# An LSTM kernel on Trainium2: the additions of its 32-step cycle laid out anew, and a head of 48 steps with a tail of 16

## The chip, the cores and the metric

The kernel runs on one core of one Trainium2 chip. A core has four compute engines that the document names as the profile does: PE (matrix multiplication, with its weight loads listed as PEld), DVE, ACT and POOL. The queue SP issues nearly all DMAs. PE writes its results to a memory of its own, PSUM; all engines reach the main on-chip memory, SBUF. The metric is the device time of one execution in microseconds; the lower, the better.

## The reference

One LSTM layer runs over 512 steps for a batch of 32, with 512 inputs and 512 hidden units, all in float32; the input is added to the output at the end:

```python
xW = jnp.einsum('ntd,dg->ntg', x, Wx) + b      # x: 32 x 512 x 512, Wx: 512 x 2048
def step(carry, xw_t):
    prev_h, prev_c = carry
    a = xw_t + prev_h @ Wh                      # Wh: 512 x 2048
    i, f, o = sigmoid of the first three quarters of a; g = tanh of the last
    next_c = f * prev_c + i * g
    next_h = o * jnp.tanh(next_c)
(_, _), hs = jax.lax.scan(step, (h0, c0), jnp.swapaxes(xW, 0, 1))
return x + jnp.swapaxes(hs, 0, 1)
```

The products `prev_h @ Wh` have to be done one step after the other. The products `x @ Wx` depend on no step and can be done at any time before the step that uses them.

## The kernel before, in words

**A step.** The loop `for k in range(T)` at the end of the kernel writes out the order of all work by hand; every engine keeps the order in which its instructions are issued. Step k first issues `h_part(k)`, the 64 matmuls `prev_h @ Wh` (line L745), which add onto gate sums in PSUM. Then comes one *window* of other work, number v = k + 4, and then `cell(k)`: three activations on ACT (L782 to L784), three DVE instructions (L785 to L787), the last tanh on ACT (L788), the product h = o * tanh(c) on DVE (L789), and its transpose on DVE (L790), for which the next `h_part` waits. POOL adds the residual (L843) and the result is stored. ACT copies the x products of the next steps into the gate banks (`seed_first`, L730, and `seed_last`).

**The x products.** Steps are taken in rows of eight (`ROW`). The first row is multiplied directly (`direct`, L660, and `keep_direct`, L676). Four rows at a time, 32 steps, form a cycle of `PER` = 32 windows. For one cycle the product `x @ Wx` is made by a fast scheme with R = 26 block products; each block product is in turn made of seven smaller ones (two levels of sums, like Strassen's). `A_OPS` holds the sums of rows ("nodes", L398), `C_OPS` the sums of products that give the 16 output blocks in `C_OF`. Each of the seven smaller products is a group of eight matmuls (L463), issued by `products(v)`. The factors of the weights are made during the head and kept in DRAM; `fetch` loads them into two rings, wa and wb (tags `wa`, `wb`), for each product. The function `begin(n)` says in which window of the cycle product n begins; it spans a few windows, so each window issues groups of several products: six groups in most windows, five in some. Four to five windows after its beginning, `finish_product` takes the two halves of a product out of PSUM.

**The sums on DVE.** In `evacuate(v)`, ACT copies parts of the products in the works (L492, L496, L505, L506) and DVE adds others (L499, L507). Sums of finished products come in two kinds. *Half adds* (L619, 128x512) are issued at once, in the window in which a half of a product is ready; these read the half in PSUM. A product that is used later as well (`copied`) is copied to SBUF by ACT in two halves (L607). *Full adds* (L635, 128x1024) read SBUF only and are put in a queue, `due`, with the window by which they must be done. A set `at_half` holds the sums that are made as half adds: those that read a product just finished, what these feed, and those whose limit leaves less than two windows. `limit` goes back from the outputs: `SLACK` gives, for each of the four rows of a cycle, how many windows after the last product its sums may be done. A sum lives in a *slot*; `slot` takes one from the list `free`, `used` gives it back after the last use. Finished outputs are stored to DRAM (`store`), and `load_xw` loads them back three steps ahead of their use; POOL adds the bias (`add_bias`, L707).

The queue `due` also holds the node sums (L398, 128x512) and the four short adds of each product (L426 to L429, 128x128). `run_due(v, room)` walks it in order: what is due by window v is issued in any case, what is due later only while `room`, counted in columns plus `FIXED` for each instruction, lasts:

```python
            if window > v and (columns + FIXED > room or not ready(v)):
                i += 1
                continue
            assert ready(window)
            due.pop(i)
            fn()
            room -= columns + FIXED
```

It is called three times in a window: twice in `evacuate`, with `FIRST_SUMS` ahead of the finishing of products and with at most `BETWEEN` ahead of the last copies, and once after it with what remains of `ROOM`. `AHEAD` says how many windows ahead of a product's beginning its sums enter the queue.

**Head and tail.** The first `HEAD` = 40 steps are the head. Its rows 1 to 4 are made by a simpler seven-product scheme, four *units* a row, 14 groups each; a window holds one unit or none, and the units are spread over the windows before `START` = 21, in which the first cycle begins. `LEAD` = 23 sets `START`: a cycle's first window is issued in step HEAD - LEAD of the first cycle, LEAD steps ahead of the first step that uses it (`START = windows_of(HEAD - LEAD)[0]`). `NSB` = 14 cycles follow. The last `TAIL` = 24 steps are multiplied directly, in quarters of a step (`tail_products`): one quarter a window at first, then two and three in turn (`2 + v % 2`), 96 in all. From step `HALVES` = 466 on, when the cycles' products are done, the step itself runs in two halves (`h_halves`, L759, and `cell_halves`, L804 to L830).

## Time and profile before

| | |
|---|---|
| three runs | 3178.97, 3179.61, 3184.61 us |
| their median | 3179.61 us |
| the profiled execution | 3181.38 us |
| its span | 3179.4 us |
| granted PE clock over the span | 1.00 |
| PE busy | 3114.2 us, 98% of the span |
| DVE busy | 2404.0 us, 76% |
| ACT busy | 1645.9 us, 52% |
| POOL busy | 1065.0 us, 33% |

The span runs from the first instruction of the profiled execution to its last. Times are in microseconds unless marked ns. Engine names stand as above; L12 is line 12 of the kernel. A line of a list of instructions gives the start, the duration, the engine, the line, the operation, what it writes and reads ("out<-in"), and the shapes as partitions x elements; "x8" stands for eight like instructions in a row, and a bracket at the end names what the engine waited for. In a table of groups, the busy time, the mean of one in ns, the idle time just ahead and what ended most of it follow the bar. In a table of windows, each engine has its busy time and count, and the last three columns are the granted clock, the share of the DMA engines and GB/s.

### The profile page before, as it was taken

To read this page: it belongs to the slowest core of one execution; us is meant where nothing else is said; L and a number is where in the kernel's file an instruction comes from. 1 tells how busy PE (TensorE), PEld (TensorE's weight loads), DVE (VectorE), ACT (ScalarE), POOL (GpSimd) and SP (SyncE) were. 2 spreads that over 40 slices of the span, in tenths; PEclk is the share of its full clock that TensorE was granted. 3 is DMA by queue.
4 is the path that set the end of the run, shared out by engine and by line. 5 is a ranking of instruction groups with operands and counts; after the bars stand their busy time and mean duration, and the time that the engine had idled before them with its cause. 6 is when DMAs were issued, how large, how long until landed. Compare 5 with 4: busy or idle time off the path is not lost.

```text
span 3179.4 us, 133096 instructions
## 1 busy us (share of the span) xinstructions
PE 3114.2 (98%) x55992; PEld 1977.0 (62%) x55992; DVE 2404.0 (76%) x6428; ACT 1645.9 (52%) x5090; POOL 1065.0 (33%) x993
## 2 busy tenths in 40 slices
PE   9999999999999999999999999999999999999998
PEld 5666666565665656666566665666666666666555
DVE  6747877878777787787877878788787877878444
ACT  2455455554555555555555555555555555554333
POOL 0223333333333333333333333333333333333310
PEclk9999999999999999999999999999999999999999
DMA  8756767767676686766867767676676767767200
GB/s 288 254 189 209 250 213 226 237 211 255 210 247 218 216 259 202 252 216 213 263 196 254 221 216 251 210 250 222 216 254 210 249 217 227 236 213 240 88 29 25
DMA packets 338853, 687.71 MB, mean 216 GB/s; under 512 B 44368, under 2 KB 112976, under 8 KB 337744
## 3 DMA queue, kind: packets, MB, share of 16 engines
q1 hardware_dynamic: 338112, 679.20, 66.1%
q8 instruction: 441, 7.23, 0.9%
q14 instruction: 156, 1.28, 0.1%
q10 hardware_dynamic: 144, 0.01, 0.0%
HBM read 499.46 MB, written 179.57 MB: 214 GB/s over the span
## 4 chain that ended last, share of the span: by engine, by line
PE 76%; DVE 15%; DMA 5%; issue 2%; ACT 2%; SPq 0%; DVEq 0%; ACTq 0%
PE gates L745 39%; PE pp L463 12%; PE acc L463 12%; PE gates L759 5%; PE p L463 4%; DVE raw_sb L619 3%; DVE t L619 2%; DMA wb<-keep_b 2%; PE pp L660 2%; DMA xw<-xw 1%; DMA wa<-keep_a 1%; DVE t L635 1%; DVE c L787 1%; DVE slot_h L619 1%; PE acc L660 1%
## 5 line engine op out<-in xcount | busy, mean ns | idle before, releaser
L745 PE MATMUL gates<-wh_sb,ht 128*32 128x384 f32 (+1 forms) x29760 | 1703.5, 379 | 20.1 <-DVE ht L790 18.4
L745 PEld LDWEIGHTS gates<-wh_sb,ht 128*32 128x32 f32 x29760 | 1022.5, 110 | 719.9 <-issue 603.9
L843 POOL TENSOR_TENSOR oc<-xr,ht 128x128 f32<-128x128 f32 x509 | 407.5, 801 | 2015.6 <-DVE ht L790 1749.1
L707 POOL TENSOR_TENSOR xw<-xw,bias_sb 128x512 f32<-128x512 f32 x480 | 673.4, 1403 | 82.0 <-DMA xw<-xw 57.3
L782 ACT ACTIVATE s<-gates 128x256 f32<-128x256 f32 x466 | 180.0, 386 | 554.5 <-PE gates L745 553.9
L785 DVE TENSOR_TENSOR fc<-s,c 128x128 f32<-128x128 f32 x465 | 139.9, 301 | 222.1 <-ACT s L782 221.3
L463 PE MATMUL pp<-wb,nodes 128*32 128x256 f32 x3808 | 304.7, 379 | 0.0
L505 ACT COPY pp<-pu 128x512 f32<-128x512 f32 x380 | 228.4, 601 | 101.2 <-DVE t L619 38.3
L789 DVE TENSOR_TENSOR fc<-s,ig 128x128 f32<-128x128 f32 x466 | 137.4, 295 | 175.9 <-ACT ig L788 175.9
L788 ACT ACTIVATE ig<-c 128x128 f32<-128x128 f32 x466 | 144.9, 311 | 179.6 <-DVE c L787 153.5
L463 PE MATMUL acc<-wb,s 128*32 128x256 f32 x2576 | 206.7, 381 | 22.8 <-DVE s L428 22.8
L730 ACT COPY gates<-xw 128x384 f32<-128x384 f32 x462 | 218.5, 473 | 4.5 <-DVE nodes L676 3.0
L507 DVE TENSOR_TENSOR pp<-acc,p 128x256 f32<-128x256 f32 x380 | 161.7, 425 | 68.5 <-ACT pp L506 65.1
L784 ACT ACTIVATE s<-gates 128x128 f32<-128x128 f32 x466 | 129.8, 279 | 157.1 <-PE gates L745 157.1
L463 PE MATMUL acc<-wa,s 128*32 128x256 f32 x2576 | 205.9, 381 | 2.4 <-DVE pp L507 0.8
L506 ACT COPY pp<-acc 128x256 f32<-128x256 f32 x380 | 136.8, 360 | 134.9 <-DVE t L619 60.9
L463 PE MATMUL pp<-wb,s 128*32 128x256 f32 x2576 | 205.4, 379 | 0.0
L463 PE MATMUL p<-wa,s 128*32 128x256 f32 x2576 | 204.7, 379 | 0.0
L499 DVE TENSOR_TENSOR pu<-acc,p 128x256 f32<-128x256 f32 x380 | 157.6, 415 | 35.9 <-ACT p L496 26.2
L790 DVE STREAM_TRANSPOSE ht<-fc 128x128 f32<-128x128 f32 x466 | 145.2, 312 | 49.7 <-DVE fc L789 1.4
L759 PE MATMUL gates<-wh_sb,ht 128*32 128x256 f32 x2944 | 168.5, 379 | 10.2 <-DVE fc L810 9.4
L759 PEld LDWEIGHTS gates<-wh_sb,ht 128*32 128x32 f32 x2944 | 114.7, 110 | 72.9 <-ACT s L806 20.4
(217 smaller groups left out, 4647.4 us busy)
## 6 DMA issues: line engine op xcount, KB each, us to landing
wb<-keep_b SPq DMA_DIRECT2D x322, 512.0 KB, 5.4
wa<-keep_a SPq DMA_DIRECT2D x322, 384.0 KB, 4.2
xw<-xw SPq DMA_DIRECT2D x480, 256.0 KB, 4.4
xw<-t SPq DMA_DIRECT2D x312, 128.0 KB, 3.1
xw<-raw_sb SPq DMA_DIRECT2D x288, 128.0 KB, 3.2
xr<-in_x_dram SPq DMA_DIRECT2D x256, 128.0 KB, 3.2
out_dram<-oc SPq DMA_DIRECT2D x255, 128.0 KB, 2.8
row<-in_x_dram SPq DMA_DIRECT2D x63, 512.0 KB, 6.9
```

Of the source, the lines that this page charges most:

```text
L463: nc.tensor.matmul(dst[t * B : (t + 1) * B], a[:, t], w, start=s in (1, 5) and m == 0, stop=True, skip_group_check=True,)
L499: nc.vector.tensor_add(job.pu[:, 1], job.acc, job.p5)
L505: nc.scalar.copy(job.pp[0], job.pu)
L507: nc.vector.tensor_add(job.pp[1][:, 1], job.acc, job.p5)
L619: add(v)(sums[sb, v][:, half], source(a), source(b))
L707: nc.gpsimd.tensor_add(xw[t], xw[t], bias_sb)
L730: nc.scalar.copy(gates[t % 2][:, 0:IFG], xw[t][:, 0:IFG])
L745: nc.tensor.matmul(g[j * B : (j + 1) * B, cols], state["ht"][:, k, :], wh_sb[:, k, j, cols], start=False, stop=True, skip_group_check=True,)
L759: nc.tensor.matmul(bank_half(m)[j * B : (j + 1) * B], state["ht"][:, k, :], half(wh_sb[:, k, j], m), start=False, stop=True, skip_group_ch ...
L782: nc.scalar.activation(s[:, 0:2], g[:, 0:2], AF.Sigmoid)
L790: nc.vector.transpose(ht.rearrange("p q b -> p (q b)"), h)
L843: (nc.gpsimd if t < T - 3 else nc.vector).tensor_add(state["oc"][:, tt % 2], xr[t][:, tt % 2], ht)
```

## The change

The change touches how the additions are laid out and how the 512 steps are divided; the matmuls of a cycle, their order and the step's own code stay.

- `HEAD` goes from 40 to 48 steps and `TAIL` from 24 to 16. The number of cycles stays 14. The head gets four more units (row 5); the tail has 64 quarter products for 96, and takes two a window throughout.
- `LEAD` goes from 23 to 28, so that `START` becomes 24 (HEAD - LEAD + 4), `LAST` 470 for 467 and `HALVES` 469 for 466. A cycle begins five steps earlier, counted from the steps that use it.
- `COPIED` names the last three products of a cycle, 23, 24 and 25. They are copied to SBUF by ACT whether or not a later sum needs that, and sums that read them are no longer made as half adds for that reason.
- `SLACK` goes from [1, 1, 1, 3] to [3, 3, 5, 8]: the outputs of the four rows may be done later after the last product of their cycle. Together with `COPIED`, this leaves 48 half adds and 18 full adds in a cycle, for 60 and 12, and three products more are copied out, 13 for 10.
- A sum may take the slot of an operand that it uses up (`last_use`, `moved`): it is then written over that operand, and needs no free slot.
- `run_due` returns what it spent, and `evacuate` counts that against the window's room, where it had counted the whole of `FIRST_SUMS` or `BETWEEN`. `ROOM` goes from 3400 to 4300, `FIRST_SUMS` from 1000 to 1200, `BETWEEN` from 1200 to 1300, and `AHEAD` from 3 to 5.
- In a cycle, `load_row` is issued eight windows ahead, where it was six; the tail loads two rows, where it loaded three.

```diff
--- before.py
+++ after.py
@@ -35,21 +35,22 @@
 R = len(A_OF)
 
 PER = ROW * MO
-HEAD = 5 * ROW
-TAIL = 3 * ROW
+HEAD = 6 * ROW
+TAIL = 2 * ROW
 NSB = (T - HEAD - TAIL) // PER
 END = HEAD + NSB * PER
 assert END + TAIL == T
 
-LEAD = 23
+LEAD = 28
 NODES = 10
 FIXED = 160
-ROOM = 3400
-FIRST_SUMS = 1000
-BETWEEN = 1200
+ROOM = 4300
+FIRST_SUMS = 1200
+BETWEEN = 1300
 HEAD_ROOM = 5000
-SLACK = [1, 1, 1, 3]
-AHEAD = 3
+COPIED = (23, 24, 25)
+SLACK = [3, 3, 5, 8]
+AHEAD = 5
 def rows_by_use():
     found = []
 
@@ -348,17 +349,18 @@
 
     def run_due(v, room):
 
-        i = 0
+        i = spent = 0
         while i < len(due):
             window, _, columns, fn, ready = due[i]
-            if window > v and (columns + FIXED > room or not ready(v)):
+            if window > v and (columns + FIXED > room - spent or not ready(v)):
                 i += 1
                 continue
             assert ready(window)
             due.pop(i)
             fn()
-            room -= columns + FIXED
+            spent += columns + FIXED
             i = 0
+        return spent
 
     nodes, node_uses = {}, {}
     node_pairs = [const.tile([P, 2, ROW, 2, B], F32, name=f"nodes_{i}") for i in range(NODES // 2)]
@@ -479,9 +481,7 @@
                     job.release()
 
     def evacuate(v, room):
-        before = len(due)
-        run_due(v - 0.5, FIRST_SUMS)
-        taken = FIRST_SUMS if len(due) < before else 0
+        taken = run_due(v - 0.5, FIRST_SUMS)
         for half, late in ((1, 5), (0, 4)):
             job = jobs.get(v - late)
             if job:
@@ -500,8 +500,7 @@
             taken += C + FIXED
         job = jobs.get(v - 3)
         if job:
-            run_due(v, min(room - taken, BETWEEN))
-            taken += BETWEEN
+            taken += run_due(v, min(room - taken, BETWEEN))
             nc.scalar.copy(job.pp[0], job.pu)
             nc.scalar.copy(job.pp[1][:, 0], job.acc)
             nc.vector.tensor_add(job.pp[1][:, 1], job.acc, job.p5)
@@ -551,7 +550,7 @@
         uses[a] += 1
         uses[b] += 1
         for v, other in ((a, b), (b, a)):
-            if v < R and (v != n or other == v):
+            if v < R and (v != n or other == v or n in COPIED):
                 copied.add(v)
     for v in C_OF:
         uses[v] += 1
@@ -561,7 +560,7 @@
     at_half = set()
     for v in range(len(ready) - 1, R - 1, -1):
         n = ready[v]
-        if n in C_OPS[v - R][1:] or any(ready[u] == n and (u in at_half) for u in users[v]):
+        if (n in C_OPS[v - R][1:] and n not in COPIED) or any(ready[u] == n and (u in at_half) for u in users[v]):
             at_half.add(v)
 
     def done_at(n):
@@ -576,17 +575,27 @@
         )
         if v not in at_half and limit[v] < done_at(n) + 2:
             at_half.add(v)
-    sums, left_uses = {}, {}
+    sums, left_uses, moved = {}, {}, set()
+
+    def last_use(sb, v):
+        return [u for u in (C_OPS[v - R][1:] if v >= R else ()) if left_uses.get((sb, u)) == 1 and u not in C_OF]
 
     def slot(sb, v):
-        sums[sb, v] = free.pop(0)
+        ends = last_use(sb, v)
+        if ends:
+            sums[sb, v] = sums[sb, ends[0]]
+            moved.add((sb, ends[0]))
+        else:
+            sums[sb, v] = free.pop(0)
         left_uses[sb, v] = uses[v]
 
     def used(sb, v):
         if (sb, v) in left_uses:
             left_uses[sb, v] -= 1
             if left_uses[sb, v] == 0:
-                free.append(sums.pop((sb, v)))
+                f = sums.pop((sb, v))
+                if (sb, v) not in moved:
+                    free.append(f)
 
     def put_out(sb, v):
         for at, u in enumerate(C_OF):
@@ -641,7 +650,8 @@
                     START + PER * sb + limit[v] - 0.5,
                     8 * P,
                     go,
-                    lambda at, v=v: len(free) > (at < START + PER * sb + limit[v] - 0.5) and all((sb, u) in sums for u in C_OPS[v - R][1:]),
+                    lambda at, v=v: all((sb, u) in sums for u in C_OPS[v - R][1:])
+                    and (last_use(sb, v) or len(free) > (at < START + PER * sb + limit[v] - 0.5)),
                 )
             return taken
 
@@ -691,7 +701,7 @@
         for t in whole:
             keep_direct(t, tail_banks[(t - END) % 6], tail_room())
         whole.clear()
-        room = 1 if v <= LAST + 3 else 2 + v % 2
+        room = 1 if v <= LAST + 3 else 2
         for t, q in pieces[:room]:
             direct(t, tail_banks[(t - END) % 6], (q,))
             if q == NJ - 1:
@@ -908,7 +918,7 @@
         if job and job.w >= START and streamed(job.kind[1]):
             job.ring[1] = rpool.tile([P, 4, C], F32, name=f"wb_{job.w}", tag="wb", bufs=4)
             nc.sync.dma_start(out=job.ring[1].rearrange("p n c -> p (n c)"), in_=kept[B_AT[job.kind[1]]][1])
-        if v in (LAST - 4, LAST - 2, LAST):
+        if v in (LAST - 4, LAST - 2):
             load_row(END // ROW + (v - LAST + 4) // 2)
         for i in [i for i in range(8) if i not in RESIDENT][2 * (v - LAST) - 2 : 2 * (v - LAST)] if v > LAST else ():
             if i in again:
@@ -917,7 +927,7 @@
             else:
                 raw[i] = rpool.tile([P, 4, C], F32, name=f"raw_again_{i}", tag="wb", bufs=4)
             nc.sync.dma_start(out=raw[i].rearrange("p n c -> p (n c)"), in_=wx[i])
-        sb, rest = divmod(v + 6 - START, PER)
+        sb, rest = divmod(v + 8 - START, PER)
         if v + 6 in UNIT_AT[2 * NJ :: NJ]:
             load_row(3 + UNIT_AT[2 * NJ :: NJ].index(v + 6))
         if rest < MO and 0 <= sb < NSB:
```

## The prediction

> **What bounds the kernel now.** I read the page, then the span in three stretches, then one cycle step by step.
>
> ```profile
> span 3179.4 us, 133096 instructions
> PE 3114.2 (98%) x55992; PEld 1977.0 (62%) x55992; DVE 2404.0 (76%) x6428; ACT 1645.9 (52%) x5090; POOL 1065.0 (33%) x993
> PE 76%; DVE 15%; DMA 5%; issue 2%; ACT 2%; SPq 0%; DVEq 0%; ACTq 0%
> 53.60:186.30 132.70, 132.70 (x2468) 90.25 (x2463) 79.09 (x182) 60.89 (x179) 27.23 (x29) 1.00 0.73 232
> 186.30:2919.30 2733.00, 2684.69 (x49156) 1715.70 (x49148) 2169.99 (x5667) 1476.03 (x4431) 990.69 (x896) 1.00 0.71 228
> 2919.30:3179.40 260.10, 245.00 (x3748) 146.17 (x3744) 119.58 (x504) 100.01 (x461) 46.91 (x64) 0.99 0.20 60
> ```
>
> PE looks full, yet DVE holds 15% of the chain that ended last. The three stretches (length, then busy PE, PEld, DVE, ACT, POOL, clock, DMA) are the head, the 14 cycles (195.2 us each) and the tail.
>
> A step is PE's h products and, in a cycle, six or five groups of eight product matmuls (seven groups for each of 26 products, 182 a cycle). L789 marks each cell.
>
> ```profile
> 1518.40 0.31 DVE L790 STREAM_TRANSPOSE ht<-fc 128x128 f32<-128x128 f32 x1
> 1519.58 3.66 PE L745 MATMUL gates<-wh_sb,ht 128*32 128x384 f32 x64
> 1523.03 0.64 PE L463 MATMUL pp<-t,row 128*32 128x256 f32 x8
> ...
> 1525.62 0.86 PE L745 MATMUL gates<-wh_sb,ht 128*32 128x384 f32 x8
> 1347.42 0.29 DVE L789 TENSOR_TENSOR fc<-s,ig 128x128 f32<-128x128 f32 x1 [0.38 <-ACT ig L788]
> 1367.21 0.29 DVE L789 TENSOR_TENSOR fc<-s,ig 128x128 f32<-128x128 f32 x1 [0.38 <-ACT ig L788]
> 1375.37 0.29 DVE L789 TENSOR_TENSOR fc<-s,ig 128x128 f32<-128x128 f32 x1 [0.38 <-ACT ig L788]
> 1386.73 0.29 DVE L789 TENSOR_TENSOR fc<-s,ig 128x128 f32<-128x128 f32 x1 [0.38 <-ACT ig L788]
> 1392.78 0.29 DVE L789 TENSOR_TENSOR fc<-s,ig 128x128 f32<-128x128 f32 x1 [0.38 <-ACT ig L788]
> ```
>
> PE's prices are 3.45 for the h products (1523.03 - 1519.58) and 0.4317 for a group (2.59 for the six up to 1525.62). A cycle's floor is 32 x 3.45 + 182 x 0.4317 = 189.0 us; a step's is 6.04 with six groups, 5.61 with five. The quiet step from 1386.73 to 1392.78 takes 6.05: at the floor. I number a cycle's windows 0 to 31; the cell at 1367.21 is that of window 1. The four windows 31, 0, 1 and 2 take 1375.37 - 1347.42 = 27.95, the last of them 8.16, against floors of 5.61 + 3 x 6.04 = 23.73. There DVE's bulk of additions sets the step, as window 12 shows:
>
> ```profile
> 1428.17 0.29 DVE L789 TENSOR_TENSOR fc<-s,ig 128x128 f32<-128x128 f32 x1 [0.38 <-ACT ig L788]
> 1428.57 0.31 DVE L790 STREAM_TRANSPOSE ht<-fc 128x128 f32<-128x128 f32 x1
> 1428.81 1.19 DVE L635 TENSOR_TENSOR raw_sb<-raw_sb,t 128x1024 f32<-128x1024 f32 x1
> 1429.92 1.48 DVE L635 TENSOR_TENSOR t<-raw_sb,slot_h 128x1024 f32<-128x1024 f32 x1
> 1431.32 0.68 DVE L619 TENSOR_TENSOR t<-pp,slot_h 128x512 f32<-128x512 f32 x1
> ...
> 1433.95 0.28 DVE L785 TENSOR_TENSOR fc<-s,c 128x128 f32<-128x128 f32 x1
> ...
> 1435.13 0.29 DVE L789 TENSOR_TENSOR fc<-s,ig 128x128 f32<-128x128 f32 x1 [0.38 <-ACT ig L788]
> ```
>
> From the end of L790 (1428.88) to L785 (1433.95) lie 5.07 us of work; the cell with its transpose takes the other 1.89 of the 6.96 from L789 to L789. So a step takes the larger of PE's floor and DVE's work + 1.89. A quiet step has slack in front: ht is there at 1518.71, PE takes it at 1519.58, 0.87 later; about 0.75 of that can be used up once before PE waits.
>
> Busy time hides part of the loss, as the ends of pipelined matmuls are counted: 2733.0 - 2684.7 = 48 us idle, but 2733.0 - 14 x 189.0 = 87 above the floor. I go by the floor. The Trainium skill (Trainium Kernel Development and Optimization, Performance Expectations) calls matmul busy time "a bad metric" for the distance to the best; by busy time the most to be gained in the cycles would be 48 us.
>
> **The change part by part.** *Sums.* Walking the queue of due sums through one cycle, before and after: products copied by ACT 10 and 13, half adds 60 and 48, full adds 12 and 18; node sums (18), short adds (104), L499 and L507 (26 each) stay. The first window behind a full add shows the prices:
>
> ```profile
> 1387.12 0.31 DVE L790 STREAM_TRANSPOSE ht<-fc 128x128 f32<-128x128 f32 x1
> 1387.36 1.18 DVE L635 TENSOR_TENSOR slot_h<-slot,t 128x1024 f32<-128x1024 f32 x1
> 1388.46 0.41 DVE L499 TENSOR_TENSOR pu<-acc,p 128x256 f32<-128x256 f32 x1
> 1388.80 0.28 DVE L428 TENSOR_TENSOR s<-row 128x128 f32<-128x128 f32 x1
> 1388.99 1.38 DVE L427 TENSOR_TENSOR s<-s,nodes 128x128 f32<-128x128 f32 x1
> 1390.29 0.28 DVE L429 TENSOR_TENSOR s<-row,s 128x128 f32<-128x128 f32 x1
> 1390.49 0.28 DVE L428 TENSOR_TENSOR s<-nodes 128x128 f32<-128x128 f32 x1
> 1390.70 0.42 DVE L507 TENSOR_TENSOR pp<-acc,p 128x256 f32<-128x256 f32 x1
> ...
> 1388.83 1.40 POOL L707 TENSOR_TENSOR xw<-xw,bias_sb 128x512 f32<-128x512 f32 x1
> ...
> 1559.45 0.69 DVE L619 TENSOR_TENSOR raw_sb<-raw_sb,t 128x512 f32<-128x512 f32 x1
> 1560.06 0.68 DVE L398 TENSOR_TENSOR nodes<-row 128x512 f32<-128x512 f32 x1
> L607 ACT COPY t<-pp 128x512 f32<-128x512 f32 x116 | 67.6, 583 | 57.7 <-PE pp L463 56.3 <-DMA wb<-keep_b 1.4
> ```
>
> From one start to the next: full add 1.11, half add and node sum 0.61, short add 0.20, L499 or L507 0.34. DVE saves 12 x 0.61 and pays 6 x 1.11: 0.7 us a cycle less. What counts is where the work lies.
>
> A sum written over its own operand: no row has its price. Between 0 and 0.3 a full add (the 1.48 of 1429.92 against 1.19), 0 to 5 us a cycle; a gain is excluded, as the same elements pass. I take 0, the nearest row being the plain add.
>
> One short add, at 1388.99, lasts 1.38 while POOL's bias add L707 runs; an add that reads a product in PSUM (L619 from pp) does not lengthen. So an add with both inputs in SBUF can wait some 1.1 us for POOL, and the change turns PSUM adds into SBUF adds. I keep 1.1 for each window in which two or more short adds follow a node or full add. The Trainium skill has this as a rule (SBUF — State Buffer, Who interferes with whom): a DVE instruction with two SBUF inputs contends with a GpSimd instruction that reads SBUF, and the one fully blocks. By that rule, the trace agrees.
>
> DVE's work after, from the walk. Window 1: node, three shorts, L507, full: 2.7 + 1.1 + 0.3 for POOL's L843 = 4.1. Window 2: full, L499, four shorts, full: 3.4 + 1.1 = 4.5. Window 3: node, L499, four shorts, L507, full: 4.3. Window 4, one short fewer: 4.1. Windows 5 and 6: full, L499, three shorts, L507, full: 3.5 + 1.1 = 4.6 each. Windows 31 and 0 fall to 3.0 and 3.5. So windows 1 to 6 need 26.2 + 6 x 1.89 = 37.5 against floors of 5 x 6.04 + 5.61 = 35.8; less the slack 0.75, 1.0 us stays. In the middle of the cycle a full add joins window 13: windows 11 to 15 hold 4.1, 4.3, 4.7, 4.5, 4.2 = 21.8, with the cells 31.3, against 29.3; less 0.75, 1.2 stays. Every other window holds at most 4.1, and 6.04 - 1.89 = 4.15 fit.
>
> One loss goes with the longer lead. A bias add that came late sat on a cell:
>
> ```profile
> 1540.91 1.29 POOL L707 TENSOR_TENSOR xw<-xw,bias_sb 128x512 f32<-128x512 f32 x1 [3.38 <-ACT s L783]
> ...
> 1541.07 1.27 DVE L787 TENSOR_TENSOR c<-fc,ig 128x128 f32<-128x128 f32 x1
> ```
>
> L787 takes 0.29 elsewhere (the rows' form is the cell's), so 0.98 was lost. Rows of xw are stored as little as 2 windows ahead of their load, after the change 7. What is late next: full adds at the end of a window whose stores hold the one SP queue, and with it the next xw load. Between 0 and 2 us a cycle; I take 0.9, about one such add.
>
> *ACT.* Six copies more, 583 ns each: 3.5 us a cycle, in windows 0 to 3. ACT is busy 1476 of 2733 us, and window 5, with two copies of its own, keeps the floor (the 6.05 above). Cost 0; with that cover gone, up to 3.5 x 14 = 49 us.
>
> *Queues and buffers.* SP issues the same stores, some later; the row load moves two windows ahead, to windows where its buffer's last reader is three windows back. The banks of the last products are freed by ACT's copy, no later than by the adds. ROOM, FIRST_SUMS, BETWEEN and AHEAD only place what is counted above. Cost 0.
>
> *Cycles:* 14 x (189.0 + 1.0 + 1.2 + 0.9) + 4.3 (ten groups that the head leaves over, as now) = 2693.7, against 2733.0.
>
> *Head.* 20 steps for 17 and four units more, 56 groups: 3 x 3.45 + 56 x 0.43 = 34.5. PE is busy 132.7 of its 132.7 us, so nothing covers this. The head ends at 186.3 + 34.5 = 220.8.
>
> *Tail.* 64 quarter products for 96, two to a step.
>
> ```profile
> 3136.55 3.66 PE L759 MATMUL gates<-wh_sb,ht 128*32 128x256 f32 x64
> 3141.72 3.66 PE L759 MATMUL gates<-wh_sb,ht 128*32 128x256 f32 x64
> 3146.55 3.66 PE L759 MATMUL gates<-wh_sb,ht 128*32 128x256 f32 x64 [1.17 <-DVE fc L810]
> ```
>
> A step with two quarters takes 5.17; one with none 4.83, where PE waits for the cell. After: 6.6 and 6.4 for the two steps with the last full adds, 5.6, 30 x 5.17, ten unfilled at 4.85, and 3.4 from the last tanh to the end: 225.6, against 260.1. Head and tail cancel.
>
> Sum: 220.8 + 2693.7 + 225.6 = 3140.1 of span. The profiled execution of before took 3181.38 for its span of 3179.4; the median of its runs is 3179.61, 0.2 above that span. Forecast 3140.
>
> **The rivals.** *Nothing is left over the floor* (0.15): full adds keep POOL back, its bias add comes at another place, and no short add waits. Unlocked, no window holds more than 4.0. Then 220.8 + 14 x 189.0 + 4.3 + 225.6 = 3097. Against it: the 1.38 above.
>
> *Late bias adds* (0.08): the stores at window ends make L707 late three times more a cycle, 0.98 each on a cell: 3 x 0.98 x 14 = 41, so 3181, no change; the change does not do what it says. For it: SP is one queue, in order. Against: the margin of 7 windows.
>
> *POOL's lock takes the gain* (0.09), which ends slower. Short adds move from the front of a window to behind node and full adds, where L707 runs. Work without waiting is 98.8 us a cycle (104 x 0.20 + 66 x 0.61 + 18 x 1.11 + 52 x 0.34), 3.09 a window, 4.98 with the cell; 195.2 / 32 = 6.10 is reached at 1.12 of waiting in every window. At a whole L707 (1.29) everywhere a cycle is 200.6 and the kernel takes 3256. Against: in the window quoted three of four short adds wait for nothing.
>
> **How the numbers follow.** The forecast has 0.68, with 3112 to 3170 as its own range (0.1 to 4.3 us a cycle above or below its 192.1, by the bounds of lock and late stores). The range 3097 to 3176 reaches to the first rival and leaves out the third and most of the second. 0.2% (6 us) is about what a measurement of this kernel can tell. Faster 0.68 + 0.15 + 0.02 = 0.85, same 0.05, slower 0.10, the small parts from the second rival's edges.
>
> **What would show it.** Right: the four windows 31 to 2 near 24.5 instead of 27.95; windows 5 and 6 longer than now, near 6.5; 48 half and 18 full adds a cycle; a cycle near 192; no bias add on a cell. Wrong: short adds above 1 us in most windows; L707 starting beside L785 to L789; L782 late behind ACT's copies in windows 0 to 3; steps of the head above 3.45 + 0.43 a group.

## The result, and the profile after

The changed kernel takes 3135.5 us (median of four runs, 3133.65 to 3136.97), where the kernel before took 3181.5 beside it: a ratio of 0.9855, with a 95% interval from 0.9838 to 0.9872. That is 1.45% faster. The forecast was 3140 and the range 3097 to 3176. The number came out; of the reasons given for it, half did not, as the experiments show.

The page of the changed kernel (first lines, and the chain's shares by engine), and then its span in the same three stretches as in the prediction (length, busy PE, PEld, DVE, ACT, POOL, clock, DMA share, GB/s). The lines of the code have moved: L755 is the old L745, L799 the old L789, L717 the bias add L707, L628 the half adds L619, L644 the full adds L635.

```profile
span 3135.0 us, 133350 instructions
PE 3101.0 (99%) x56184; PEld 1986.8 (63%) x56184; DVE 2421.7 (77%) x6337; ACT 1697.0 (54%) x5186; POOL 1030.9 (33%) x1001
PE 76%; DVE 18%; ACT 3%; issue 2%; DMA 1%; DVEq 0%; SPq 0%; ACTq 0%
```

```profile
53.20:220.90 167.70, 167.70 (x3115) 100.92 (x3108) 89.42 (x215) 77.06 (x222) 35.67 (x35) 1.00 0.66 207
220.90:2906.30 2685.40, 2672.49 (x49143) 1736.00 (x49136) 2187.74 (x5588) 1515.63 (x4509) 940.17 (x896) 1.00 0.72 232
2906.30:3135.00 228.70, 208.94 (x3316) 128.39 (x3307) 109.37 (x460) 95.72 (x436) 54.82 (x66) 1.00 0.23 72
```

The head ends at 220.9 (186.3 before), the tail takes 228.7 (260.1), and the 14 cycles take 2685.4 (2733.0). So all of the gain is in the cycles, 47.6 us, and head and tail together give 3.2 of it back. DVE is busier than before and holds 18% of the chain for 15%. Busy time does not tell its work, as it counts waits for POOL too (see the end); by the prediction's prices the new sums are 0.7 us a cycle less work, and a cycle became 3.5 us shorter.

The timeline of DVE and POOL in one cycle: the cells of windows 30, 2 and 4, and window 5, some rows left out, up to its own cell at 1405.38.

```profile
1362.91 0.29 DVE L799 TENSOR_TENSOR fc<-s,ig 128x128 f32<-128x128 f32 x1 [0.38 <-ACT ig L798]
...
1387.01 0.29 DVE L799 TENSOR_TENSOR fc<-s,ig 128x128 f32<-128x128 f32 x1 [0.37 <-ACT ig L798]
...
1398.97 0.29 DVE L799 TENSOR_TENSOR fc<-s,ig 128x128 f32<-128x128 f32 x1 [0.38 <-ACT ig L798]
1399.37 0.31 DVE L800 STREAM_TRANSPOSE ht<-fc 128x128 f32<-128x128 f32 x1
1399.60 1.18 DVE L644 TENSOR_TENSOR slot_h<-slot_h,raw_sb 128x1024 f32<-128x1024 f32 x1
1400.70 0.41 DVE L499 TENSOR_TENSOR pu<-acc,p 128x256 f32<-128x256 f32 x1
1401.04 0.28 DVE L431 TENSOR_TENSOR s<-row,s 128x128 f32<-128x128 f32 x1
1401.23 1.38 DVE L430 TENSOR_TENSOR s<-nodes 128x128 f32<-128x128 f32 x1
...
1403.07 1.21 DVE L644 TENSOR_TENSOR t<-t,t 128x1024 f32<-128x1024 f32 x1
...
1405.38 0.29 DVE L799 TENSOR_TENSOR fc<-s,ig 128x128 f32<-128x128 f32 x1 [0.37 <-ACT ig L798]
...
1399.76 1.35 POOL L853 TENSOR_TENSOR oc<-xr,ht 128x128 f32<-128x128 f32 x1 [3.50 <-DVE ht L800]
1401.07 1.39 POOL L717 TENSOR_TENSOR xw<-xw,bias_sb 128x512 f32<-128x512 f32 x1
```

Windows 31 to 2 take 1387.01 - 1362.91 = 24.10 us, where they took 27.95 (24.34 and 27.96 in the mean of the cycles). Window 5 takes 6.41 and has become longer (6.05 before): it now holds two full adds and a short add that lasts 1.38 beside POOL's L717. The full adds at 1399.60 and 1403.07 are written over an operand and last 1.18 and 1.21. A row leaves the numbers of the buffers out; by the order in which the code takes its slots, 14 of the 18 full adds of a cycle are written so, and their median is 1.21 us, that of the others 1.20.

For every run below, the same reading of all cycles: the mean cycle (the 2nd to the 14th, from cell to cell) and what its windows take above PE's floor of 5.61 or 6.04. These numbers are worked out from the starts of the cell's product o * tanh(c), L799 or its line in each trace; a window that gains back a little stands below zero. Windows 17 to 26, left out, lie within 0.1 us of the floor in all, but 0.4 below it in e6 and e7. Each ratio is to the kernel before as it ran beside that kernel, and each cycle comes from one trace.

| kernel | time, us | ratio to before | cycle, us | above the floor in windows 30 to 2 | 3 to 10 | 11 to 16 | 27 to 29 | head ends | tail |
|---|---|---|---|---|---|---|---|---|---|
| before | 3179.6 | 1 | 195.07 | 4.86 | -0.24 | 1.43 | 0.02 | 186.3 | 260.1 |
| changed | 3135.5 | 0.9855 | 191.59 | 0.92 | 0.50 | 1.08 | 0.03 | 220.9 | 228.7 |
| e1_room_old | 3181.2 | 1.0001 | 195.16 | 0.38 | 0.03 | 5.59 | 0.14 | 221.0 | 228.5 |
| e2_not_copied | 3136.7 | 0.9855 | 191.59 | 0.81 | 0.59 | 1.08 | 0.10 | 220.8 | 227.3 |
| e3_no_bias | 3100.9 | 0.9747 | 189.07 | 0.01 | 0.03 | 0.02 | 0.02 | 220.9 | 225.6 |
| e4_before_lead | 3185.2 | 1.0013 | 195.11 | 4.79 | -0.16 | 1.44 | 0.01 | 220.9 | 230.0 |
| e5_before_room | 3157.1 | 0.9930 | 193.29 | 2.66 | -0.17 | 1.78 | 0.01 | 186.6 | 260.2 |
| e6_spread | 3127.6 | 0.9835 | 191.03 | 0.42 | -0.06 | 2.06 | 0.05 | 220.7 | 228.0 |
| e7_spread_early | 3115.3 | 0.9798 | 189.99 | 0.23 | -0.14 | 1.05 | 0.25 | 221.1 | 228.4 |
| e8_lead23 | 3133.6 | 0.9855 | 191.78 | 0.70 | 0.84 | 1.21 | 0.02 | 240.2 | 204.5 |
| e9_early | 3134.2 | 0.9852 | 191.45 | 0.67 | 0.43 | 1.27 | 0.07 | 220.8 | 228.7 |
| e10_best | 3113.6 | 0.9787 | 189.84 | 0.03 | 0.03 | 0.77 | 0.01 | 220.9 | 227.9 |
| e11_before_queue | 3184.9 | 1.0006 | 195.57 | 1.90 | 0.20 | 1.14 | 3.33 | 186.3 | 259.2 |
| e12_queue_rows | 3137.2 | 0.9864 | 191.93 | 1.55 | 0.30 | 1.06 | 0.03 | 186.2 | 259.1 |

### The profile page after: what moved, and what is told of

Read it like the earlier page. It is cut to its first block, busy times and chain, and to the rows that moved or that the text cites. A ratio compares the mean times of both kernels' runs of the same rounds, so it can differ in the third digit from the quotient of the medians.

```text
span 3135.0 us, 133350 instructions
## 1 busy us (share of the span) xinstructions
PE 3101.0 (99%) x56184; PEld 1986.8 (63%) x56184; DVE 2421.7 (77%) x6337; ACT 1697.0 (54%) x5186; POOL 1030.9 (33%) x1001
## 3 DMA queue, kind: packets, MB, share of 16 engines
q8 instruction: 442, 7.24, 1.0%
## 4 chain that ended last, share of the span: by engine, by line
PE 76%; DVE 18%; ACT 3%; issue 2%; DMA 1%; DVEq 0%; SPq 0%; ACTq 0%
PE gates L755 39%; PE pp L465 13%; PE acc L465 13%; PE p L465 4%; PE gates L769 4%; DVE t L644 2%; DVE s L430 1%; DVE t L628 1%; DVE raw_sb L644 1%; DVE c L797 1%; ACT ig L798 1%; DVE ht L800 1%; DVE fc L799 1%; PE pp L670 1%; DVE s L428 1%
## 5 line engine op out<-in xcount | busy, mean ns | idle before, releaser
L755 PE MATMUL gates<-wh_sb,ht 128*32 128x384 f32 (+1 forms) x29952 | 1714.5, 380 | 12.0 <-DVE ht L800 9.5
L755 PEld LDWEIGHTS gates<-wh_sb,ht 128*32 128x32 f32 x29952 | 1026.0, 110 | 718.5 <-issue 600.8
L853 POOL TENSOR_TENSOR oc<-xr,ht 128x128 f32<-128x128 f32 x509 | 406.0, 798 | 1997.3 <-DVE ht L800 1794.7
L717 POOL TENSOR_TENSOR xw<-xw,bias_sb 128x512 f32<-128x512 f32 x488 | 640.5, 1313 | 89.9 <-DMA xw<-xw 53.4
L799 DVE TENSOR_TENSOR fc<-s,ig 128x128 f32<-128x128 f32 x469 | 138.3, 295 | 176.3 <-ACT ig L798 176.3
L795 DVE TENSOR_TENSOR fc<-s,c 128x128 f32<-128x128 f32 x468 | 140.8, 301 | 143.8 <-ACT s L792 141.8
L769 PE MATMUL gates<-wh_sb,ht 128*32 128x256 f32 x2752 | 157.5, 379 | 14.7 <-DVE fc L820 14.7
L496 ACT COPY p<-p 128x256 f32<-128x256 f32 x384 | 146.4, 381 | 28.0 <-PE p L465 25.8
```

What stands on the lines that cost most here:

```text
L717: nc.gpsimd.tensor_add(xw[t], xw[t], bias_sb)
L755: nc.tensor.matmul(g[j * B : (j + 1) * B, cols], state["ht"][:, k, :], wh_sb[:, k, j, cols], start=False, stop=True, skip_group_check=True,)
L769: nc.tensor.matmul(bank_half(m)[j * B : (j + 1) * B], state["ht"][:, k, :], half(wh_sb[:, k, j], m), start=False, stop=True, skip_group_ch ...
L799: nc.vector.tensor_mul(h, s[:, 3], tc_t)
L853: (nc.gpsimd if t < T - 3 else nc.vector).tensor_add(state["oc"][:, tt % 2], xr[t][:, tt % 2], ht)
```

## The experiments

### What holds the rest: POOL's bias add

```diff
-            if 2 * 4 - 2 <= k and k + 2 < END:
+            if 2 * 4 - 2 <= k and k + 2 < HEAD:
                 add_bias(k + 2)
```

> The changed kernel without the bias add on POOL (L717) for the steps that the cycles feed; it leaves out the bias of these steps, so the output differs from the reference by that. Theory of the prediction (what stays above PE's floor in windows 1 to 6 and 11 to 16, now 2.6 us a cycle, is DVE's adds blocked while L717 runs): a cycle falls to about 189.1 and the time by 14 x 2.5 = 35 us to 3100 us. Rival (the rest is DVE's work itself, L717 and the adds only happen together): a cycle stays within 0.5 us of 191.6 and the time within 7 us of 3135.5.

3100.9 us, 0.9747 of before (0.9730 to 0.9763). The cycles and the tail of this run, and a window 5 of it:

```profile
220.90:2873.50 2652.60, 2652.14 (x49144) 1760.37 (x49139) 2020.19 (x5589) 1521.26 (x4510) 402.20 (x473) 1.00 0.73 235
2873.50:3099.10 225.60, 209.22 (x3316) 128.30 (x3306) 106.52 (x460) 96.01 (x436) 21.79 (x41) 1.00 0.24 73
```

```profile
1385.09 0.29 DVE L799 TENSOR_TENSOR fc<-s,ig 128x128 f32<-128x128 f32 x1 [0.38 <-ACT ig L798]
...
1387.36 0.28 DVE L430 TENSOR_TENSOR s<-nodes 128x128 f32<-128x128 f32 x1
...
1390.86 0.29 DVE L799 TENSOR_TENSOR fc<-s,ig 128x128 f32<-128x128 f32 x1 [0.38 <-ACT ig L798]
```

The short add that took 1.38 takes 0.28, the window 5.77 for 6.41, and every cycle from the 2nd on falls to 189.07, 0.1 over PE's floor, in all groups of windows of the table. The tail falls by 3.1 as well, to the 225.6 of the prediction. So the whole rest above the floor goes with the bias add. It could also have held up ACT's copies of xw into the gate banks, which read what it writes; but in the changed kernel these waited for it only 1.7 us in all, in 2 places. What remains is that it keeps DVE out. The Trainium skill (SBUF — State Buffer, Who interferes with whom) calls what the two share an exclusive lock; the trace agrees, 1.38 against 0.28.

### What carries the gain: the kinds of sums, or the room

The first run takes only the room back, the second only the three copied products.

```diff
-ROOM = 4300
-FIRST_SUMS = 1200
-BETWEEN = 1300
+ROOM = 3400
+FIRST_SUMS = 1000
+BETWEEN = 1200
```

> The changed kernel with the room of a window as it was before: ROOM 3400, FIRST_SUMS 1000, BETWEEN 1200 (what is spent is still counted exactly). Theory of the prediction (the gain comes from the sums of the last three products, the longer SLACK and the longer lead; the room only places work, cost 0): the time stays at 3135.5 us, within 6 us, and a cycle at 191.6. Rival, the room: with 3400 spent and counted, the full adds no longer fit ahead of their limits and pile up at them. Walking the queue at the prediction's prices gives a pile in windows 11 to 14 (8.5, 6.6, 7.3, 7.1 us) and a cycle of about 194.3, which is 14 x 2.6 = 36 us more: 3172 us.

```diff
-COPIED = (23, 24, 25)
+COPIED = ()
```

> The changed kernel with COPIED empty: products 23 to 25 are no longer copied out, and their sums are half adds again (60 half and 12 full adds a cycle); room, SLACK and lead stay changed. Theory of the prediction (these half adds are what made windows 31 to 2 long): they fall into windows 1 to 4 again and cost at least half of what windows 31 to 2 gained (3.6 us a cycle), so 14 x 1.8 = 25 us more: about 3160 us. Rival, the room: which kind of add it is makes little difference as long as the others can be moved away from them; the walk of the queue gives 192.1 for 192.0 a cycle: 3137 us, no difference that can be measured, with windows 3 and 4 near 6.7 and windows 5 and 6 near 6.0 and 5.5.

With the old room the time is 3181.2, a ratio of 1.0001 (0.9991 to 1.0010): the gain is gone. Without the three copies it is 3136.7, a ratio of 0.9855 (0.9840 to 0.9869): nothing has changed. Window 11 of the run with the old room:

```profile
1449.18 0.29 DVE L799 TENSOR_TENSOR fc<-s,ig 128x128 f32<-128x128 f32 x1 [0.38 <-ACT ig L798]
...
1449.82 1.18 DVE L644 TENSOR_TENSOR slot_h<-slot_h,raw_sb 128x1024 f32<-128x1024 f32 x1
1450.92 1.48 DVE L644 TENSOR_TENSOR raw_sb<-t,raw_sb 128x1024 f32<-128x1024 f32 x1
1452.44 2.19 DVE L644 TENSOR_TENSOR t<-t,slot_h 128x1024 f32<-128x1024 f32 x1
...
1457.68 0.29 DVE L799 TENSOR_TENSOR fc<-s,ig 128x128 f32<-128x128 f32 x1 [0.38 <-ACT ig L798]
...
1451.28 2.26 POOL L717 TENSOR_TENSOR xw<-xw,bias_sb 128x512 f32<-128x512 f32 x1
```

Three full adds that found no room before their limit stand in one window of 8.50 us; the third meets L717 and lasts 2.19. Windows 30 to 2 are at the floor in this run (0.38 above it), just as the prediction's account of the sums would have it, and all of it comes back in windows 11 to 16 (5.59). The rival's walk had 8.5, 6.6, 7.3 and 7.1 for windows 11 to 14; in the mean they took 8.35, 6.70, 7.54 and 6.99 (its 3172 us in all was 9 short). The work that left one crowded place stood in another.

That the second run had other sums is seen in the counts of the half adds of the cycles, of the changed kernel first and then of this run (the columns are those of the stretches, with DVE's L628 alone):

```profile
220.90:2910.00 2689.10, 452.79 (x672) 1.00 0.72 232
```

```profile
220.90:2910.00 2689.10, 571.76 (x832) 1.00 0.72 232
```

119 us of half adds more, in place of some 94 us of full adds, and the same mean cycle of 191.59. The new SLACK and the in-place slots stay in this run.

### The lead

```diff
-HEAD = 5 * ROW
-TAIL = 3 * ROW
+HEAD = 6 * ROW
+TAIL = 2 * ROW
@@
-LEAD = 23
+LEAD = 28
@@
-        room = 1 if v <= LAST + 3 else 2 + v % 2
+        room = 1 if v <= LAST + 3 else 2
@@
-        if v in (LAST - 4, LAST - 2, LAST):
+        if v in (LAST - 4, LAST - 2):
```

> The kernel before with HEAD 48, TAIL 16, LEAD 28 and two quarter products a window in the tail; queue, room, SLACK and kinds of adds as before. Theory of the prediction: head and tail cancel, and the longer lead takes away the late bias adds, 0.9 us a cycle: 14 x 0.9 = 13 us less, 3167 us, a cycle of 194.2, and no bias add on a cell. First rival: the lead does nothing, late bias adds cost nothing that stays: 3180 us. Second rival: head and tail don't cancel and carry a part of the gain: below 3160 us with a cycle still at 195.

The opposite, on the changed kernel:

```diff
-LEAD = 28
+LEAD = 23
```

> The changed kernel with LEAD 23 for 28 (START 29, HALVES 474; outputs are then stored as little as two windows ahead of their load). Theory of the prediction (the longer lead takes away late bias adds, 0.9 us a cycle): 13 us more in the cycles, 3 to 4 less in head and tail (five steps of 4.1 more in the head, five unfilled steps of 4.85 fewer in the tail): about 3145 us, with more bias adds on a cell. Rival (the lead is worth nothing in the cycles): cycles stay at 191.6 and the time falls by the 4 us of head and tail: 3132 us.

The kernel before with the longer lead takes 3185.2, 1.0013 of before (1.0003 to 1.0022), with its old cycle of 195.11. The changed kernel with the short lead takes 3133.6, 0.9855 (0.9841 to 0.9870), with a cycle of 191.78 for 191.59. Both say that the lead is worth nothing in the cycles that can be told. A late bias add of the run with the longer lead, and what it did (POOL's and DVE's timeline, near the cell of window 30):

```profile
1380.05 1.29 POOL L707 TENSOR_TENSOR xw<-xw,bias_sb 128x512 f32<-128x512 f32 x1 [3.35 <-DMA xw<-xw]
...
1380.23 1.25 DVE L787 TENSOR_TENSOR c<-fc,ig 128x128 f32<-128x128 f32 x1
```

POOL sat idle for 3.35 us until the transfer that loads xw had landed, and the cell's sum L787 lasted 1.25 beside the bias add, as in the prediction's example, though the row of xw was stored five windows earlier than in the kernel before. Over the whole run POOL waited for these transfers 47.7 us in 44 places, where it had waited 57.3 in 47. So an earlier store does not make the load earlier; an earlier load is tried below.

### Back to the kernel before: how little of the change is needed

One number:

```diff
-ROOM = 3400
+ROOM = 4300
```

> The kernel before with one number changed: ROOM 4300 for 3400. Theory, the room (supported by the run with the old room): the sums of the last windows spread into windows that had slack; walking the queue gives a cycle of 191.4 for 194.1, window 2 at 7.8 for 8.2 and windows 31, 0 and 1 at PE's floor or near it, so 14 x 2.7 = 38 us less: about 3142 us. Rival (it takes the room together with the new kinds of sums, the in-place slots and the exact count): not below 3170 us.

All of the queue's numbers:

```diff
-ROOM = 3400
-FIRST_SUMS = 1000
-BETWEEN = 1200
+ROOM = 4300
+FIRST_SUMS = 1200
+BETWEEN = 1300
@@
-AHEAD = 3
+AHEAD = 5
@@
-        i = 0
+        i = spent = 0
@@
-            if window > v and (columns + FIXED > room or not ready(v)):
+            if window > v and (columns + FIXED > room - spent or not ready(v)):
@@
-            room -= columns + FIXED
+            spent += columns + FIXED
@@
+        return spent
@@
-        before = len(due)
-        run_due(v - 0.5, FIRST_SUMS)
-        taken = FIRST_SUMS if len(due) < before else 0
+        taken = run_due(v - 0.5, FIRST_SUMS)
@@
-            run_due(v, min(room - taken, BETWEEN))
-            taken += BETWEEN
+            taken += run_due(v, min(room - taken, BETWEEN))
```

> The kernel before with all of the queue's numbers changed (ROOM 4300, FIRST_SUMS 1200, BETWEEN 1300, AHEAD 5 and the exact count) and nothing of the sums' kinds, COPIED, SLACK, in-place slots, LEAD, HEAD or TAIL. Theory, the room: these numbers are the whole of the gain; the walk of the queue gives 191.8 a cycle for 194.1: 3135 to 3147 us, by whether late bias adds go with it. Rival (room alone is worth half, as the run with ROOM 4300 gave, and the rest comes from the new kinds of sums and the lead): 3155 us or more.

The same with the row loads of a cycle two windows earlier:

```diff
-        sb, rest = divmod(v + 6 - START, PER)
+        sb, rest = divmod(v + 8 - START, PER)
```

> The kernel of the run with all of the queue's numbers (e11_before_queue) with the row loads of a cycle issued eight windows ahead, where they were six; sums, COPIED, SLACK, slots, LEAD, HEAD and TAIL stay those of the kernel before. Theory (the queue's numbers carry the gain, and in e11_before_queue it was given back in window 28, 9.31 us, where DVE's first node sum waits for a row's transfer): window 28 falls to 6.04, 13 x 3.27 = 43 us less than 3184.9: about 3142 us. Rival (the transfer stays late, or the new kinds of sums are needed after all): 3160 us or more.

ROOM alone takes half of the way: 3157.1, 0.9930 (0.9914 to 0.9947). That met neither expectation. The walk was right on window 2 (7.8 said, 7.75 measured), but its cycle had been 1.0 us short for the kernel before already (194.1 for 195.07), and windows 12, 13 and 30 still took 7.24, 6.81 and 6.17. All of the queue's numbers together took 3184.9, 1.0006 (0.9997 to 1.0016): no gain, as the rival had it. Window 28 of that run, where a cycle lost 3.3 us (the lines lie two above those of the kernel before, so that L787 is the product o * tanh(c) here):

```profile
1329.27 0.29 DVE L787 TENSOR_TENSOR fc<-s,ig 128x128 f32<-128x128 f32 x1 [0.38 <-ACT ig L786]
1329.67 0.31 DVE L788 STREAM_TRANSPOSE ht<-fc 128x128 f32<-128x128 f32 x1
1333.09 0.69 DVE L399 TENSOR_TENSOR nodes<-row 128x512 f32<-128x512 f32 x1 [3.11 <-DMA row<-in_x_dram]
```

With AHEAD 5 and room to spare, the first node sum of the next cycle now comes before its row has landed, and DVE, which keeps its order, waits 3.11 us with everything else behind it. With the row loads two windows earlier the window is back at its floor and the kernel takes 3137.2, 0.9864 (0.9848 to 0.9880): the time of the whole change, within what can be told. Its three stretches:

```profile
53.10:186.20 133.10, 133.10 (x2475) 90.57 (x2468) 82.70 (x183) 61.26 (x180) 30.05 (x29) 1.00 0.72 231
186.20:2876.20 2690.00, 2675.98 (x49145) 1735.03 (x49140) 2160.05 (x5668) 1477.82 (x4430) 917.51 (x896) 1.00 0.72 232
2876.20:3135.30 259.10, 245.88 (x3760) 146.79 (x3752) 118.12 (x503) 99.87 (x461) 44.96 (x64) 1.00 0.20 62
```

So the queue's numbers and the earlier row loads are enough for the gain. ROOM alone brings half of it; which of the others brings the second half was not tried. The copied products, the new SLACK, the in-place slots, the lead and the new head and tail are not needed for it; with them a cycle is 0.3 us shorter, and head and tail are 220.9 + 228.7 = 449.6 for 186.2 + 259.1 = 445.3.

### Late transfers, and a layout that beats both kernels

The numbers of the next three kernels were looked for by walking the queue with the prediction's prices until, by that walk, no window was over full. The first, on the changed kernel (the count goes back to that of the kernel before):

```diff
-ROOM = 4300
-FIRST_SUMS = 1200
-BETWEEN = 1300
+ROOM = 4400
+FIRST_SUMS = 800
+BETWEEN = 1700
@@
-COPIED = (23, 24, 25)
+COPIED = (25,)
@@
-AHEAD = 5
+AHEAD = 6
```

> The changed kernel with other numbers for the same queue: ROOM 4400, FIRST_SUMS 800, BETWEEN 1700, AHEAD 6, COPIED (25,), and the count of the kernel before (a call that spent anything counts as the whole of FIRST_SUMS or BETWEEN). These were chosen by walking the queue with DVE's prices and POOL's lock: no window then needs more than it has beside its neighbours, and a cycle comes to 189.1, PE's floor, with the bias add in place. Theory (the lock and the adds cost only where a window is over full): 191.6 - 189.1 = 2.5 us a cycle less, some 0.5 of it kept by late bias adds: 3135.5 - 14 x 2.0 = 3107 us. Rival (the lock costs wherever it strikes, so only leaving out the bias add can bring the floor): not below 3128 us.

The second loads xw earlier (in a pool of five buffers for four; pu has three for four):

```diff
-            if 2 * 4 - 3 <= k and k + 3 < END:
-                load_xw(k + 3)
+            if k == 2 * 4 - 3:
+                load_xw(k + 3)
+            if 2 * 4 - 3 <= k and k + 4 < END:
+                load_xw(k + 4)
```

> The kernel of the run before this one (e6_spread), with the rows of xw loaded four steps ahead of their use, where it was three (five xw buffers for four, three pu buffers for four). Theory (what remains above the floor in windows 27 and 30 is bias adds that wait for the xw transfer, which stands in SP's queue behind other transfers): those windows fall to the floor, 0.4 us a cycle, 5 us in all against e6_spread. Rival (these windows lose by the stores and row loads themselves, or the transfer is late by more than a step): no difference to e6_spread.

e6_spread took 3127.6 (0.9835, 0.9821 to 0.9850), 20 us over the theory and, within what can be told, as the rival had it (not below 3128). In its window 11, 7.42 us long, the trace shows one place where the floor was not reached (L720 is the bias add here):

```profile
1431.73 2.32 POOL L720 TENSOR_TENSOR xw<-xw,bias_sb 128x512 f32<-128x512 f32 x1 [1.87 <-DMA xw<-xw]
...
1432.82 1.37 DVE L431 TENSOR_TENSOR s<-nodes,s 128x128 f32<-128x128 f32 x1
```

POOL waits 1.87 us for the transfer, and the bias add, held up by DVE and holding DVE in turn, lies in the middle of the adds. With the earlier load the kernel took 3115.3 (0.9798, 0.9783 to 0.9812), 12 us less, more than the 5 expected, and below what the rival of e6_spread allowed with the bias add in place: the crowded windows 11 to 16 gained too, 2.06 to 1.05. What then stood out was window 27, 7.2 us in half of the cycles. There, with AHEAD 6, the first node sum waited 0.6 to 1.8 us for its row's transfer, as in e11_before_queue, and in six of seven cases was then held up by the bias add.

The earlier load on the changed kernel alone:

> The changed kernel with the rows of xw loaded four steps ahead of their use, where it was three (five xw buffers for four, three pu buffers for four), and nothing else. Theory (bias adds that come late do so because the xw transfer stands in SP's queue behind other transfers, whatever the lead is): windows 27 and 30 fall to the floor, 0.4 us a cycle, and some of windows 2 and 3 with them: 5 to 10 us less than the changed kernel, about 3128 us. Rival (late bias adds cost nothing more in the changed kernel, they were a matter of the tighter layout of e6_spread): 3135.5 us.

3134.2 us (0.9852, 0.9837 to 0.9867), no difference to the changed kernel's 3135.5 that can be told, as the rival had it. POOL waited for xw transfers in the changed kernel (its L717, idle time by what ended it), and no longer does in this run, where no such line is left:

```profile
  DMA xw<-xw: 53.4, 42
```

The late bias adds did lie on cells in the changed kernel. The cell's first product L795 in the changed kernel and then in this run, with the least, the median and the greatest ns:

```profile
L795 DVE TENSOR_TENSOR fc<-s,c x468: 272/292/1179, 60.4 to 2905.1; 128x128 f32<-128x128 f32 x156
L795 DVE TENSOR_TENSOR fc<-s,c x468: 271/291/296, 60.3 to 2903.2; 128x128 f32<-128x128 f32 x156
```

Of all instructions of the cells on DVE, 14 are lengthened in the changed kernel, all beside L717, by 8.9 us together; in the kernel before 11 were, by 9.0 us; in this run none is. Yet the late transfers cost little in time: 0.14 us a cycle (191.59 to 191.45). Window 27 gives back in window 28 all that it loses (6.50 and 5.61 us, for 6.04 each), window 30 a part.

The last one joins the two lessons: earlier xw rows as in e9_early, no node sum ahead of its row, and no window over full by the walk.

```diff
-ROOM = 4300
-FIRST_SUMS = 1200
-BETWEEN = 1300
+ROOM = 3750
+FIRST_SUMS = 1100
+BETWEEN = 2200
@@
-COPIED = (23, 24, 25)
-SLACK = [3, 3, 5, 8]
-AHEAD = 5
+COPIED = (25,)
+SLACK = [3, 3, 5, 6]
+AHEAD = 4
```

> The changed kernel with early rows of xw as in e9_early and ROOM 3750, FIRST_SUMS 1100, BETWEEN 2200, AHEAD 4, SLACK [3, 3, 5, 6], COPIED (25,), with the exact count kept. The walk of the queue gives 189.1 a cycle, and the node sums no longer reach ahead of the row loads (in e7_spread_early, with AHEAD 6, window 27 waited for a row in half of the cycles). Theory (full windows, late transfers and the lock together are all that stands above the floor): a cycle of 189.3 to 189.8, 3100 to 3110 us. Rival (some 1 us a cycle stays whatever the layout): 3115 us, as e7_spread_early.

3113.6 us, 0.9787 (0.9773 to 0.9802) of the kernel before and clear of the changed kernel's interval. The cycles:

```profile
220.90:2883.10 2662.20, 2658.61 (x49143) 1750.31 (x49136) 2142.46 (x5627) 1493.63 (x4456) 930.93 (x896) 1.00 0.73 234
```

A cycle takes 189.84, and what is left above the floor lies in windows 11 to 16 (0.77, window 12 above all, 6.97 us). The time is 4 us over what the theory allowed and not told from e7_spread_early, as the rival had it. Window 12 of the seventh cycle shows what the theory left out:

```profile
1432.06 0.69 DVE L628 TENSOR_TENSOR slot<-pp,raw_sb 128x512 f32<-128x512 f32 x1 [1.49 <-ACT t L616]
...
1430.89 1.28 POOL L717 TENSOR_TENSOR xw<-xw,bias_sb 128x512 f32<-128x512 f32 x1
```

DVE waits 1.49 us there for ACT's copy of a product, and its adds come behind that. The bias add falls almost whole into this idle time, so it is not what makes the window long. The bias add is still on POOL and still keeps DVE out: of the 32.8 us that leaving it out takes from the cycles (2685.4 to 2652.6), 23.2 come here from the layout and the earlier load together (2685.4 to 2662.2).

## Why the prediction was right, and where it was not

- *The bound.* Right for this change: PE's floor of 189.0 us a cycle is reached to 0.1 when DVE is not held up (189.07 in e3_no_bias). That a step takes the larger of PE's floor and DVE's work + 1.89 leaves out that DVE can also wait for its inputs: 1.49 us for a copy in e10_best, 3.11 us for a row in e11_before_queue.
- *The sum.* Head 220.9 for 220.8. Cycles 2685.4 for 2693.7: 191.6 a cycle for 192.1. Tail 228.7 for 225.6. The terms that were off are the late bias adds (0.9 us a cycle taken, 0.14 measured by e9_early) and the first steps of the tail, where the steps of 6.6, 6.4 and 5.6 did not count the bias add in them: without it the tail is 225.6. Cycles forecast 8.3 us too long and a tail 3.1 too short cancel in part, which brings the sum nearer than its terms. Two figures that the forecast does not hang on are off: the third rival comes to 3259 with the 4.3 us of the ten groups, not 3256, and the range of 3112 to 3170 is 2 us a cycle either way, which 0.1 to 4.3 does not give.
- *Sums.* The step that failed. The counts were right (48 and 18), the prices too (an in-place full add costs what another does, 1.21 for 1.20), and so were the windows that the walk gave: 24.3 for "near 24.5", 6.42 and 6.50 for "near 6.5" in the mean. The prediction also said that what counts is where the work lies. But it told the gain as one of the sums, of half adds that become full adds, and wrote of ROOM, FIRST_SUMS, BETWEEN and AHEAD that they only place what is counted, cost 0. Placing was all but 0.3 of a cycle's 3.5 us. e1_room_old, with the new sums in the old room, gains nothing; e2_not_copied, with the old kinds of sums in the new room, loses nothing; e12_queue_rows has the gain without the new sums. The walk had the room in it, so the number was right for a reason that the text gave to another part of the change: as far as the cause goes, that was luck.
- *The lead.* Failed. It was said to take the late bias adds away; e4_before_lead and e8_lead23 show no gain from it. Of the signs of being right, "no bias add on a cell" did not come: L717 lengthens the cell in 14 steps, where it had been 11. What takes it away is loading xw a step earlier (e9_early), so POOL waits for the late load and not for a late store; what holds the load up was not tried.
- *Row loads, cost 0.* Right as a number, but the cover was not named: with AHEAD 5 and the row loads left where they were, a cycle loses 3.3 us in window 28 (e11_before_queue).
- *ACT, cost 0.* Right: e2_not_copied has six copies a cycle fewer and the same time.
- *POOL's lock.* Right in mechanism and size: 2.2 us a cycle was forecast, 1.0 for windows 1 to 6 and 1.2 for windows 11 to 15. Leaving the bias add out brings 2.5; windows 30 to 10 had 1.4 of it and windows 11 to 16 1.1.
- *Head and tail cancel.* Nearly: they cost 3.2 us here and 4.5 in e4_before_lead.

Of the rivals, "nothing is left over the floor" did not come in the changed kernel, but it is what e3_no_bias shows, at 3100.9 for its 3097. The other two did not come: late bias adds are there but cost 0.14 us a cycle, and short adds wait in some windows, not in every one.

## What to carry to other kernels

When a change moves both what work there is and where it is put, predict each alone: a walk of the whole can give the right time and the wrong reason, and two runs that take one part back each tell them apart. Where an engine has slack in some steps and too much work in others, as DVE here, the budget per step can decide more than the cheapness of the work; and work that may now run earlier needs its inputs earlier too. A wait that can't be removed may be moved to a step that has room for it, as 23.2 of 32.8 us were here.

## What the runs showed of the hardware that was not expected

- Waiting for POOL counts as DVE's busy time. Without the bias add DVE was busy 2020.2 us in the cycles, with it 2187.7, for the same adds: they lasted 167.6 us longer, 12 a cycle, of which only 2.5 a cycle reached the end of a step.
- Adds that read a product in PSUM are not held up. In the changed kernel the median of the half adds that read one is 0.68 us whether L717 runs beside them or not; half adds from SBUF alone last 1.26 beside it, and 0.69 where it did not run (kernel before).
- It works both ways: the residual add on POOL (L853) lasts 1.35 at 1399.76 beside DVE's full add, and 0.46 where DVE is all but idle, as here in e6_spread (L856 there):

```profile
1442.26 0.46 POOL L856 TENSOR_TENSOR oc<-xr,ht 128x128 f32<-128x128 f32 x1 [3.38 <-DVE ht L803]
```
